# A cross-attention kernel on one core: setup and the first two batches in another order, the first keys by block products

## The chip, the core and the metric

The kernel runs on one core of one Trainium2 chip. A core has a matrix engine (TensorE, called PE in the profile; PEld is its loading of weights), VectorE (DVE), ScalarE (ACT), GpSimd (POOL), and SyncE (SP), which here only issues DMAs. [...] The metric is device microseconds of one execution, as the median of several runs.

## The reference, cut to what matters

Sixteen batches; x has 100 rows of 640, ctx_768 has 722 rows of 384, the last four of them "ca" tokens. All data is float32.

```python
query = hidden_states @ Wq                     # 100 x 640
keyt = enc @ Wk                                # 718 x 640
valt = enc @ Wv
hs = _mha(query, keyt, valt)                   # 8 heads of 80
ca_q1 = jnp.einsum('btc,th->bch', ca, Wq_ca)
ca_q1 = ca_q1[:, indices, :]                   # 100 rows picked
ca_hs1 = _mha(ca_q1, residual, residual)
ca_q2 = ca_hs1 @ Wq
ca_k2 = ca @ Wk_ca
ca_v2 = ca @ Wv_ca
ca_hs2 = _mha(ca_q2, ca_k2, ca_v2)
out = hs + ca_hs2
out = out @ Wout + b_out
out = out + residual
```

So there is a main attention over 718 rows, and a second one that goes through two small attentions.

## The kernel before, in words

**Block products.** The context's 718 rows are three thirds of 240 columns (u), each with three chunks of 128 features (c); a weight has three chunks and two halves (g). Keys (all but the last 128 columns, which go the plain way) and values of a batch are 3 x 3 x 2 blocks, made not by 18 products but by 15: each product f takes one sum of input blocks ("form" f, a_form) and one sum of weight blocks (W_AT), adds into a PSUM bank A to E, and what the bank then holds is copied (ACT) or added (DVE, L390) to one output block (`Blocks.go`, L381). V_PLAN and K_PLAN are the orders. `enc_sums` (L466) makes the input sums, thirteen operations on POOL for each batch. `weight_sums` (L487) makes the weight sums once, twelve operations; the five "late" ones overwrite raw weight blocks, or build on those. `Keys` and `Values` are the two uses.

**Batch 0 is special.** Its keys are made plainly, by `first_keys` (L561: four chunks of nine products, and the last chunk by `last_keys`, L568), and its values too, by `first_values` (L353), for the six blocks (i) of 120 rows. Values 1, 4, 2, 5 are made in the setup, values 3 and 0 within batch 0.

**Setup (L243 to L1080).** SP loads the context of batch 0 (`load_first`), the tokens (cat, wkca), the transposed query weight wqt, xT, the key weight wkt (five DMAs), the query weight wq (five) and wvca. PE makes first values, k2_ps (tokens' keys), m_ps (five), y_ps of batch 0, the transposes of wkt into w_ps, which DVE and ACT copy in turn to wk_sb, the keys of batch 0, va_ps (tokens' values, sent to DRAM as va_d), and the queries of batches 0 and 1 (`queries`, L515, five chunks). The second attention of a batch is the class `Second` (L703): `products` (y_ps and g), `scores1` (four products and three sums of 100x800 on POOL, into e1), `softmax1` (DVE), `exponentials1` (ACT), `softmax2` (z_ps on PE), `scores2`, `softmax3` (DVE), `load` (values vb, by POOL's DMA queue), `values2` (four products and three sums on POOL, into hs2).

**A batch (L1089 on).** `scores` in three groups of two blocks, copied by ACT into st (the first and third group sit in PSUM pairs of tag ps2, the second in psk and ps1); `most`, the largest, on DVE; `Maximum` (its steps are called by `top.go`); the values of this batch and the keys of the next, block by block, with `subtract` (DVE, 120x1600) and `exponential` (ACT) among them; `last_keys` of the next batch (L568); `a_ps`, probabilities by values, on PE; then normalisation on DVE. `Last` projects finished rows of 128 with wout: most batches end with one projection (o_ps, L923), and batches 0, 1, 5, 10 and 14 have none in that place. Odd batches also make the queries of the next two.

**What sets the order.** From L1088 on a manual schedule holds: each of the five engines gets its instructions in the order in which they are written. Ahead of it the framework's scheduler orders instructions by its own model of when their inputs are ready, within the limits given by `in_order` and `issue_after`. Tiles of one tag share buffers, and a new one waits until the last reader of the old is done.

Of the kernel before, what the change touches and what calls it, by code (L numbers as in the profile page):

```python
# [8 lines left out]
F32 = mybir.dt.float32  # L9
AF = mybir.ActivationFunctionType  # L10
ALU = mybir.AluOpType
# [113 lines left out]
def kernel(  # L125
# [84 lines left out]
    def rest_tile(name):  # L210
        return main.tile([P, len(A_REST), KT], F32, tag="rest", name=name)
# [11 lines left out]
    def load_rest(b, enc):  # L223
        rest = rest_tile(f"rest_{b}")
        for (u, c), i in A_REST.items():
            nc.sync.dma_start(
                out=rest[:, i], in_=enct[b][:, c, u * (KT - 1) : u * (KT - 1) + KT]
            )
        return enc[0], rest
# [44 lines left out]
    load_first(0, CC, 1, slice(KN, KT))  # L274
    for u in (2, 0):
        load_first(0, CC, u, slice(0, KT))
    tokens = vb_tile("tokens")
    cat_sb = tokens[:, CC, : CC * B * T].rearrange("p (c n) -> p c n", c=CC)
    wkca_sb = tokens[:, :CC, :]
    in_order(nc.sync.dma_start(out=cat_sb, in_=cat.rearrange("p c b t -> p c (b t)")))  # L280
    in_order(nc.sync.dma_start(out=wkca_sb, in_=wkca.rearrange("(c p) n -> p c n", p=P)))
    wqt_sb = wout_sb
    wkt_sb = kT.rearrange("p c u k -> p c (u k)")
    in_order(nc.sync.dma_start(out=wqt_sb, in_=wqt.rearrange("(c p) r -> p c r", p=P)))
    xT = inp.tile([P, 2, HC, S], F32, tag="xT", name="xT_0")
    in_order(nc.sync.dma_start(out=xT, in_=xt[0:2].rearrange("b p c s -> p b c s")))
    for c in range(HC):
        in_order(nc.sync.dma_start(out=wkt_sb[:, c, :CAD], in_=packed(wkt, c)))  # L288
# [197 lines left out]

    def weight_sums(engine, w, late):  # L487

        at = lambda f: w[:, W_AT[f]]
        raw = lambda c, g: w[:, 2 * (c - 1) + g - 1]  # L490
        for out, left, right in (
            (at(5), raw(2, 2), raw(1, 2)),
            (at(14), raw(2, 1), raw(2, 2)),
            (at(7), raw(3, 2), at(5)),
            (at(3), raw(1, 1), at(7)),
            (at(13), raw(3, 1), at(7)),
        ) if late else (
            (at(0), raw(1, 2), raw(1, 1)),
            (at(1), raw(2, 1), raw(3, 1)),
            (at(2), raw(1, 1), raw(2, 2)),  # L500
            (at(6), raw(2, 1), raw(1, 1)),
            (at(10), raw(3, 1), raw(2, 2)),
            (at(11), raw(2, 2), raw(3, 2)),
            (at(12), raw(3, 2), raw(3, 1)),
        ):
            engine.tensor_tensor(out, left, right, ALU.subtract)  # L506

# [6 lines left out]

    def queries(p, xT, tiles, n):  # L515
        qp, qz = tiles
        q_ps = psum(f"q_ps_{p}_{n}")
        for c in range(HC):
            nc.tensor.matmul(  # L519
                q_ps[:, : 2 * S].rearrange("p (j s) -> p j s", j=2),  # L520
                wq_sb[:, c, n * P : (n + 1) * P],
                xT[:, :, c, :],
                start=(c == 0),
                stop=(c == HC - 1),
            )
# [12 lines left out]
    def chunk_keys(n, banks, weights, enc):  # L538
# [20 lines left out]
        return copies  # L559

    def first_keys(enc):  # L561
        for n in range(HC - 1):
            banks = [psum(f"kT_ps_0_{n}_{k}") for k in range(2)]
            weights = [wk_sb[:, 2 * c + n % 2, n // 2] for c in range(CC)]
            chunk_keys(n, banks, weights, enc)
        last_keys(0, enc)

# [123 lines left out]
    def keys(m):  # L691

        for c, (_, groups) in enumerate(GROUPS):
            at = [i for i, h in enumerate(groups) if h >= 0]
            n, step = len(at), at[1] - at[0]
            nc.gpsimd.tensor_tensor(
                m2[:, c, at[0] : at[-1] + 1 : step, :],
                m(c).unsqueeze(1).to_broadcast([P, n, HT]),
                hmask[:, c, :n].unsqueeze(2).to_broadcast([P, n, HT]),
                ALU.mult,  # L700
            )

    class Second:  # L703


        def __init__(self, b, xT):
            self.b, self.xT = b, xT[:, b % 2]
            self.top = None

            self.ca = small.tile([S, T, S], F32, tag="ca", name=f"ca_{b}", bufs=2)  # L710
# [153 lines left out]
    class Last:  # L864
# [51 lines left out]
        def project(self, chunks=range(HC)):  # L916
            for r, xn in self.xn.items():
                lo, n = OC[r]
                if chunks[0] == 0:
                    self.o_ps = pair(f"o_ps_{r}")  # L920
                o_ps = self.o_ps
                for c, k in [(c, k) for k in range(2) for c in chunks]:
                    nc.tensor.matmul(  # L923
                        o_ps[:n, k, : H // 2],
                        hsTs[r][:, c, :n],
# [7 lines left out]
                if self.split:  # L933
                    for k in range(2):
                        cols = slice(k * (H // 2), (k + 1) * (H // 2))
                        nc.vector.tensor_tensor(
                            xn[:n, cols], o_ps[:n, k, : H // 2], xn[:n, cols], ALU.add
                        )
# [3 lines left out]
                nc.vector.tensor_tensor(both, o_ps[:n, :, : H // 2], both, ALU.add)  # L942
                nc.sync.dma_start(out=o_v, in_=xn[:n])
# [46 lines left out]
    for n, heads in enumerate(HEADS):  # L990
# [9 lines left out]
            ALU.mult,  # L1000
        )
    for c in range(HC):
        m_ps = psum(f"m_ps_{c}")
# [13 lines left out]
        nc.sync.dma_start(out=m_d[c], in_=m_sb[c])  # L1017
    second = Second(0, xT)
    keys(load_m(0))
    summed = second.products()  # L1020
    second.copy()
    second.scores1()
    keys(load_m(1))

    for c in range(HC):
        w_ps = psum(f"w_ps_{c}")
        for cc in range(CC):
            nc.tensor.transpose(
                w_ps[:, cc * P : (cc + 1) * P], wkt_sb[:, c, cc * P : (cc + 1) * P], ident
            )  # L1030
        (dve if c % 2 else act)(
            wk_sb[:, c % 2 : 6 : 2, c // 2] if c < HC - 1 else wk4,
            w_ps[:, : CC * P].rearrange("p (a n) -> p a n", a=CC),
        )

    with tc.issue_after(summed.ins):
        for c in range(HC):
# [11 lines left out]
            )  # L1049
    first_keys(enc)  # L1050

    va = wide("va")[:, : H // 2]
    va_ps = psum("va_ps")
    for c in range(CC):
# [10 lines left out]
    for n in range(2):  # L1065
# [3 lines left out]
        )  # L1069
    with tc.issue_after(copied.ins):  # L1070
        nc.vector.tensor_reduce(
            qmask, ident.rearrange("p (r u k) -> p u r k", r=RG, u=2), AX.XY, ALU.add
        )
    tiles = queries_tiles(0)
# [6 lines left out]
    engines = {  # L1081
        mybir.EngineType.Pool,
        mybir.EngineType.PE,
        mybir.EngineType.DVE,
        mybir.EngineType.Activation,
        mybir.EngineType.SP,
    }
    ctx.enter_context(tc.manual_schedule(engines=engines))  # L1088
    for b in range(B):  # L1089
# [63 lines left out]

        if b == 0:
            now.scores2()
            now.softmax3()
            second.scores1()
            top.go(3)
            kk.go(3)
            top.go(1)  # L1160
# [16 lines left out]
            subtract(2)  # L1177
            exponential(2)
            now.values2()
            second.load()  # L1180
            second.softmax1(4)
        elif b + 1 < B:
# [6 lines left out]

            second.scores1(seen)  # L1190
            last.load()
            top.go(3)
# [31 lines left out]
        else:  # L1224
# [23 lines left out]
            last.project()  # L1248
        if b + 2 < B:
            if b == 0:  # L1250
                enc_next = load_rest(b + 2, enc_next)
            keys(m_next)
            enc_sums(enc_next)
# [97 lines left out]
```

## Time and profile before

| what | value |
| --- | --- |
| median of 3 runs | 962.16 us (961.81 to 964.65) |
| the profiled execution: time, span | 964.32 us, 962.6 us |
| granted TensorE clock, mean | 0.995 |
| start of scores, batches 0, 1, 2 | 67.6, 111.2, 172.5 us |
| start of scores, batches 5, 6 | 342.4, 399.3 us |
| last matmul, end of span | 958.7, 962.6 us |
| DMA in the first 40 us | 0.73 to 0.97 of the engines' time |

The time from one start of scores to the next is the length of a batch, and PE is busy in nearly all of it from batch 2 on. The profile gives for each group of instructions the idle time of the engine ahead of it, and what ended it; "<- ACT st L1119" reads: until ScalarE's instruction of line 1119, which wrote st, was done.

### The profile page before, as it was taken

The page shows a single profiled execution, that of the slowest core. Times are in us where ns is not written, and L with a number is a line of the kernel's source. Part 1 is how long each engine was busy: PE and PEld are TensorE (multiplying, and loading weights), DVE is VectorE, ACT ScalarE, POOL GpSimd, SP SyncE. Part 2 cuts the span into 40 slices and gives each one's busy share as a digit, 9 for nine tenths or more (in the row PEclk, how much of TensorE's full clock was granted, in tenths as well). Part 3 has the DMA queues.
Part 4 walks back from the last instruction along what each step waited for, and adds up shares of the span by engine and source line. Part 5 has one row for each costly group of instructions (what it writes and reads, how often), then busy time and mean ns, then how long its engine had stood idle before and what let it go on. Part 6 is the DMA issues. An engine that isn't in the chain of part 4 may idle for free.

```text
span 962.6 us, 25608 instructions
## 1 busy us (share of the span) xinstructions
PE 941.2 (98%) x11215; PEld 799.9 (83%) x11215; DVE 673.1 (70%) x1083; ACT 359.1 (37%) x596; POOL 632.9 (66%) x572
## 2 busy tenths in 40 slices
PE   8898989999999999999999999999999999999998
PEld 6797869888798798978889787897879878898866
DVE  1357796696947869496874959569694786928883
ACT  1124433433424443342434334243432444325351
POOL 4269999485955768487673958738695576836613
PEclk9899999999999999999999999999999999999999
DMA  7930304022040301304050040401204031120100
GB/s 247 280 120 4 99 1 134 3 56 75 1 148 2 92 24 49 89 1 128 1 142 9 1 129 1 134 3 46 70 3 147 2 95 35 49 80 1 59 8 29
DMA packets 45256, 62.48 MB, mean 65 GB/s; under 512 B 13337, under 2 KB 37209, under 8 KB 43545
## 3 DMA queue, kind: packets, MB, share of 16 engines
q1 hardware_dynamic: 41608, 42.97, 15.1%
q0 software_dynamic: 2512, 16.72, 6.1%
q8 instruction: 88, 1.44, 0.6%
q10 hardware_dynamic: 1024, 1.15, 0.3%
q14 instruction: 24, 0.19, 0.1%
HBM read 55.26 MB, written 5.57 MB: 63 GB/s over the span
## 4 chain that ended last, share of the span: by engine, by line
PE 93%; DVE 2%; SPq 2%; DMA 2%; ACT 1%; issue 1%; ACTq 0%; DVEq 0%
PE s_ps L598 12%; PE a_ps L1272 11%; PE v_psA L419 10%; PE v_psB L419 8%; PE kT_ps L543 8%; PE k_psA L450 7%; PE q_ps L519 7%; PE o_ps L923 7%; PE k_psB L450 6%; PE v_psC L419 3%; PE k_psC L450 3%; PE v_psD L419 2%; PE v_psE L419 2%; PE y_ps L721 2%; PE k_psE L450 1%; SPq L288 1%
## 5 line engine op out<-in xcount | busy, mean ns | idle before, releaser
L756 POOL TENSOR_TENSOR e<-ca,g 100x800 f32<-100x800 f32 x64 | 99.3, 1562 | 155.4 <-DVE most L1123 118.7
L845 POOL TENSOR_TENSOR hs<-vb,p 100x640 f32<-100x640 f32 x64 | 105.6, 1660 | 42.5 <-DVE p L831 40.0
L1272 PEld LDWEIGHTS a_ps<-vs,st 120*64 120x64 f32 (+3 forms) x3072 | 109.1, 125 | 10.9 <-ACT st L1119 5.4
L852 POOL TENSOR_TENSOR hs<-hs,hs 100x640 f32<-100x640 f32 x48 | 115.3, 2402 | 3.8
L1272 PE MATMUL a_ps<-vs,st 120*64 120x81 f32 (+3 forms) x3072 | 112.5, 234 | 4.9 <-ACT st L1119 4.9
L419 PE MATMUL v_psA<-wv_sb,enc 128*120 128x320 f32 x360 | 113.2, 437 | 2.6 <-DVE wv_sb L506 2.6
L485 POOL TENSOR_TENSOR enc<-enc 128x240 f32<-128x240 f32 x135 | 103.9, 784 | 7.1
L1111 DVE TENSOR_TENSOR st<-st,over 120x1600 f32<-120x1600 f32 x48 | 108.0, 2253 | 0.0
L598 PE MATMUL s_ps<-qp,kT 32*120 32x100 f32 x3072 | 98.8, 263 | 0.7 <-issue 0.7
L598 PEld LDWEIGHTS s_ps<-qp,kT 32*120 32x120 f32 x3072 | 95.8, 179 | 2.5 <-issue 1.1
L763 POOL TENSOR_TENSOR e<-e,e 100x800 f32<-100x800 f32 x48 | 95.2, 1983 | 3.8
L615 ACT COPY st<-s_ps 120x800 f32<-120x800 f32 x64 | 49.7, 829 | 128.0 <-PE s_ps L598 128.0
L419 PE MATMUL v_psB<-wv_sb,enc 128*120 128x320 f32 x300 | 93.5, 434 | 0.0
L450 PE MATMUL k_psA<-enc,wk_sb 128*128 128x240 f32 x360 | 87.9, 367 | 2.5 <-DVE kT L390 1.4
L1283 DVE RECIPROCAL rs<-a_ps 100x4 f32<-100x4 f32 x32 | 5.8, 181 | 117.3 <-PE a_ps L1272 117.1
L419 PEld LDWEIGHTS v_psA<-wv_sb,enc 128*120 128x120 f32 x360 | 65.0, 184 | 26.0 <-issue 3.7
L450 PEld LDWEIGHTS k_psA<-enc,wk_sb 128*128 128x128 f32 x360 | 68.2, 190 | 19.9 <-DVE kT L390 1.9
L1123 DVE TENSOR_TENSOR most<-most,st 120x800 f32<-120x800 f32 x64 | 65.6, 1025 | 22.3 <-ACT st L609 21.2
L1119 ACT ACTIVATE st<-st 120x1600 f32<-120x1600 f32 x48 | 74.0, 1543 | 11.4 <-DVE st L1111 11.4
L419 PEld LDWEIGHTS v_psB<-wv_sb,enc 128*120 128x120 f32 x300 | 55.2, 184 | 22.5 <-issue 0.7
L450 PE MATMUL k_psB<-enc,wk_sb 128*128 128x240 f32 x300 | 73.0, 366 | 0.0
L485 POOL TENSOR_TENSOR enc<-enc,rest 128x240 f32<-128x240 f32 x45 | 34.7, 772 | 57.9 <-DMA rest<-in_enct 22.7
(138 smaller groups left out, 1762.5 us busy)
## 6 DMA issues: line engine op xcount, KB each, us to landing
vb<-va_d POOLq DMA_DIRECT2D x16, 1000.0 KB, 7.6
enc<-in_enct SPq DMA_DIRECT2D x30, 240.0 KB, 3.7
enc<-in_enct SPq DMA_DIRECT2D x15, 360.0 KB, 3.5
xT<-in_xt SPq DMA_DIRECT2D x8, 500.0 KB, 4.6
rest<-in_enct SPq DMA_DIRECT2D x31, 120.0 KB, 6.5
xn<-in_x SPq DMA_DIRECT2D x11, 320.0 KB, 9.2
out<-xn SPq DMA_DIRECT2D x11, 320.0 KB, 2.4
ca<-in_cas SPq DMA_DIRECT2D x16, 156.2 KB
```

Source lines behind the costliest of these rows:

```text
L419: nc.tensor.matmul(at[0][j][:KN, : H // 2], a_form(self.enc, f)[:, j * KN : (j + 1) * KN], wv_sb[:, W_AT[f]], start=first, stop=last, skip ...
L450: nc.tensor.matmul(at[:, i * KT : (i + 1) * KT], wk_sb[:, W_AT[f], i], a_form(self.enc, f), start=(first and i == 0), stop=last, skip_grou ...
L485: nc.gpsimd.tensor_tensor(out, left, right, op)
L543: nc.tensor.matmul(bank[:, i * KT : (i + 1) * KT], weights[c], a_raw(enc, u, c), start=(i == 0 and c == 0), stop=(c == CC - 1), skip_group ...
L598: nc.tensor.matmul(s_ps[r][:n, 256 * a + lo : 256 * a + hi], kT[rows, c, u, j * KN : (j + 1) * KN], rhs, start=(a == 0 and c == 0), stop=( ...
L756: first = nc.gpsimd.tensor_tensor(to, self.ca[:, t, :].unsqueeze(1).to_broadcast([S, NH, S]), g[:, :, t].unsqueeze(2).to_broadcast([S, NH, ...
L763: nc.gpsimd.tensor_tensor(e, e, to, ALU.add)
L845: first = nc.gpsimd.tensor_tensor(to, vb[:S, t, :].rearrange("p (h d) -> p h d", h=NH), p2[:, :, t].unsqueeze(2).to_broadcast([S, NH, D]), ...
L852: nc.gpsimd.tensor_tensor(sums, sums, to, ALU.add)
L1111: return nc.vector.tensor_tensor(st[i], st[i], top.over[:KN].unsqueeze(1).to_broadcast([KN, 2, ROWS]), ALU.subtract,)
L1119: nc.scalar.activation(st[i], st[i], AF.Exp, scale=SCALE)
L1272: nc.tensor.matmul(a_v[lo:hi, h % 4], st[i // 2][: KEYS[i], i % 2, h * S + lo : h * S + hi], block(i, h // 4)[: KEYS[i], h % 4], start=(i ...
```

## The change

- **Keys of batch 0** are made by `Keys(0, enc)`, the 15 block products, instead of `first_keys`: three, then va_ps, then four, then two behind each of the first four chunks of the queries; `last_keys(0)` comes ahead of the fifth chunk. The manual schedule begins ahead of them. Queries of batch 0 and va_ps use PSUM pairs.
- For this the encoder sums of batch 0 come in the setup on POOL, ahead of `scores1(0)`, and all twelve sums of key weights come on DVE ahead of the copies of the query weight, in a new order. The copies of w_ps are all ACT's. ca_0 is loaded ahead of wkt.
- **First values 0** move from batch 0 to the setup, ahead of m_ps; their context third is loaded behind cat and wkca.
- **Value weight sums**: the seven early ones go from POOL to DVE, ahead of batch 0's softmax1; the five late ones from DVE in batch 1 to POOL in batch 0.
- **Batch 0's order**: scores1 of batch 1 earlier, scores2 and softmax3 later, the mask products (`keys`) and the late sums ahead of values2, which now waits for the third subtract. The load of vb for batch 1 moves into batch 1. The rest blocks of batch 1's context get a buffer of their own kind (hsT).
- **Every batch to 14**: the third exponential is issued ahead of the last keys' copies.
- **The last output** (`split`) uses two PSUM tiles, one for each half.

```diff
     def load_rest(b, enc):
-        rest = rest_tile(f"rest_{b}")
+        if b == 1:
+            room = hsT_tile("rest_1").rearrange("p c s -> p (c s)")
+            rest = room[:, : len(A_REST) * KT].rearrange("p (i k) -> p i k", k=KT)
+        else:
+            rest = rest_tile(f"rest_{b}")
...
-    for u in (2, 0):
-        load_first(0, CC, u, slice(0, KT))
+    load_first(0, CC, 2, slice(0, KT))
...
     in_order(nc.sync.dma_start(out=wkca_sb, in_=wkca.rearrange("(c p) n -> p c n", p=P)))
+    load_first(0, CC, 0, slice(0, KT))
...
     in_order(nc.sync.dma_start(out=xT, in_=xt[0:2].rearrange("b p c s -> p b c s")))
+    ca_0 = small.tile([S, T, S], F32, tag="ca", name="ca_0", bufs=2)
+    in_order(nc.sync.dma_start(out=ca_0, in_=cas[0].unsqueeze(0).to_broadcast([S, T, S])))
...
-    def weight_sums(engine, w, late):
+    def weight_sums(engine, w, late=None):
...
+        for f, left, right in (
+            (0, raw(1, 2), raw(1, 1)),
+            (11, raw(2, 2), raw(3, 2)),
+            (12, raw(3, 2), raw(3, 1)),
+            (5, raw(2, 2), raw(1, 2)),
+            (7, raw(3, 2), at(5)),
+            (13, raw(3, 1), at(7)),
+            (1, raw(2, 1), raw(3, 1)),
+            (3, raw(1, 1), at(7)),
+            (6, raw(2, 1), raw(1, 1)),
+            (10, raw(3, 1), raw(2, 2)),
+            (2, raw(1, 1), raw(2, 2)),
+            (14, raw(2, 1), raw(2, 2)),
         ):
-            engine.tensor_tensor(out, left, right, ALU.subtract)
+            if late is None or late == (f in (5, 7, 13, 3, 14)):
+                made = engine.tensor_tensor(at(f), left, right, ALU.subtract)
+        return made
...
                 if chunks[0] == 0:
-                    self.o_ps = pair(f"o_ps_{r}")
+                    if self.split:
+                        self.o_ps = [bank(f"o_ps_{r}_{k}") for k in range(2)]
+                    else:
+                        self.o_both = pair(f"o_ps_{r}")
+                        self.o_ps = [self.o_both[:, k] for k in range(2)]
...
+    first_values(0, enc, (act, act))
     for c in range(HC):
         m_ps = psum(f"m_ps_{c}")
...
-    second = Second(0, xT)
-    keys(load_m(0))
+    second = Second(0, xT, ca_0)
+    made_keys = keys(load_m(0))
     summed = second.products()
     second.copy()
-    second.scores1()
+    with tc.issue_after(made_keys.ins):
+        enc_sums(enc)
+        second.scores1()
     keys(load_m(1))
...
-        (dve if c % 2 else act)(
+        act(
...
     with tc.issue_after(summed.ins):
+        made = weight_sums(nc.vector, wk_sb)
+
+    with tc.issue_after(made.ins):
         for c in range(HC):
...
-    first_keys(enc)
+    tiles = queries_tiles(0)
+    ctx.enter_context(tc.manual_schedule(engines=engines))
+    k0 = Keys(0, enc)
+    k0.go(3)
     va = wide("va")[:, : H // 2]
...
+    k0.go(4)
     for n in range(HC):
-        queries(0, xT, tiles, n)
+        queries(0, xT, tiles, n, bank)
+        k0.go(2)
+        if n == HC - 2:
+            last_keys(0, enc)
+    weight_sums(nc.vector, wv_sb, False)
...
         if b == 0:
+            enc_sums(enc)
             now.load()
             now.softmax1()
-            for late in (False, True):
-                weight_sums(nc.vector, wk_sb, late)
-            enc_sums(enc)
-            weight_sums(nc.gpsimd, wv_sb, False)
...
-        if b == 1:
-            weight_sums(nc.vector, wv_sb, True)
...
         if b == 0:
+            second.scores1()
+            kk.go(3)
+            top.go(3)
             now.scores2()
-            now.softmax3()
-            second.scores1()
-            top.go(3)
-            kk.go(3)
             top.go(1)
             first_values(3, e_in, (act, act), (0,), bank)
             kk.go(2)
             top.go()
             first_values(3, e_in, (act, act), (1,), bank)
             kk.go(3)
-            first_values(0, e_in, (act, act), (0,), bank)
+            now.softmax3()
             kk.go(2)
             subtract(0)
             exponential(0)
-            first_values(0, e_in, (act, act), (1,), bank)
             kk.go(2)
             subtract(1)
             kk.go(3)
             exponential(1)
             second_next, enc_next, m_next = loads()
+            less = subtract(2)
+            exponential(2)
             last_keys(b + 1, enc)
-            subtract(2)
-            exponential(2)
-            now.values2()
-            second.load()
+            enc_next = load_rest(b + 2, enc_next)
+            keys(m_next)
+            weight_sums(nc.gpsimd, wv_sb, True)
+            now.values2(less)
+            enc_sums(enc_next)
             second.softmax1(4)
...
             second.scores1(seen)
+            if b == 1:
+                now.load()
             last.load()
...
             subtract(2)
+            exponential(2)
             last_keys(b + 1, enc)
-            exponential(2)
```

More of the change, by code (lines that the diff above doesn't have):

```diff
@@ L485, in enc_sums @@
             nc.gpsimd.tensor_tensor(out, left, right, op)
-    def weight_sums(engine, w, late):
+    def weight_sums(engine, w, late=None):
         at = lambda f: w[:, W_AT[f]]
         raw = lambda c, g: w[:, 2 * (c - 1) + g - 1]
[L491 to L504, printed above, removed]
-        ):
-            engine.tensor_tensor(out, left, right, ALU.subtract)
+        for f, left, right in (
[11 more added lines that the diff above has]
+            (14, raw(2, 1), raw(2, 2)),
+        ):
+            if late is None or late == (f in (5, 7, 13, 3, 14)):
+                made = engine.tensor_tensor(at(f), left, right, ALU.subtract)
+        return made
     def queries_tiles(p):
@@ L513, in queries_tiles, with queries @@
         ]
-    def queries(p, xT, tiles, n):
+    def queries(p, xT, tiles, n, get=psum):
         qp, qz = tiles
-        q_ps = psum(f"q_ps_{p}_{n}")
+        q_ps = get(f"q_ps_{p}_{n}")
         for c in range(HC):
@@ L559, in chunk_keys @@
         return copies
[L561 to L566, printed above, removed]
     def last_keys(b, enc):
@@ L695, in keys @@
             n, step = len(at), at[1] - at[0]
-            nc.gpsimd.tensor_tensor(
+            made = nc.gpsimd.tensor_tensor(
                 m2[:, c, at[0] : at[-1] + 1 : step, :],
@@ L701, in keys, with __init__ @@
             )
+        return made
     class Second:
-        def __init__(self, b, xT):
+        def __init__(self, b, xT, ca=None):
             self.b, self.xT = b, xT[:, b % 2]
             self.top = None
+            self.ca = ca
+            if ca is not None:
+                return
             self.ca = small.tile([S, T, S], F32, tag="ca", name=f"ca_{b}", bufs=2)
@@ L923, in project @@
                     nc.tensor.matmul(
-                        o_ps[:n, k, : H // 2],
+                        o_ps[k][:n, : H // 2],
                         hsTs[r][:, c, :n],
@@ L936, in project @@
                         nc.vector.tensor_tensor(
-                            xn[:n, cols], o_ps[:n, k, : H // 2], xn[:n, cols], ALU.add
+                            xn[:n, cols], o_ps[k][:n, : H // 2], xn[:n, cols], ALU.add
                         )
@@ L941, in project @@
                 both = xn[:n].rearrange("p (k d) -> p k d", k=2)
-                nc.vector.tensor_tensor(both, o_ps[:n, :, : H // 2], both, ALU.add)
+                nc.vector.tensor_tensor(
+                    both, self.o_both[:n, :, : H // 2], both, ALU.add
+                )
                 nc.sync.dma_start(out=o_v, in_=xn[:n])
@@ L1049 @@
             )
-    first_keys(enc)
+    with tc.issue_after(copied.ins):
+        nc.vector.tensor_reduce(
+            qmask, ident.rearrange("p (r u k) -> p u r k", r=RG, u=2), AX.XY, ALU.add
+        )
+    engines = {
+        mybir.EngineType.Pool,
+        mybir.EngineType.PE,
+        mybir.EngineType.DVE,
+        mybir.EngineType.Activation,
+        mybir.EngineType.SP,
+    }
+    tiles = queries_tiles(0)
+    ctx.enter_context(tc.manual_schedule(engines=engines))
+    k0 = Keys(0, enc)
+    k0.go(3)
     va = wide("va")[:, : H // 2]
-    va_ps = psum("va_ps")
+    va_ps = bank("va_ps")
     for c in range(CC):
@@ L1069 @@
         )
[L1070 to L1074, printed above, removed]
-    for n in range(HC):
-        queries(0, xT, tiles, n)
+    k0.go(4)
+    for n in range(HC):
+        queries(0, xT, tiles, n, bank)
[3 more added lines that the diff above has]
+    weight_sums(nc.vector, wv_sb, False)
     nc.gpsimd.dma_start(out=bias, in_=bout[0].partition_broadcast(P))
@@ L1080 @@
     last, enc_next, second_next = None, load_rest(1, load_enc(1)), Second(1, xT)
[L1081 to L1088, printed above, removed]
     for b in range(B):
@@ L1248 @@
             last.project()
-        if b + 2 < B:
-            if b == 0:
-                enc_next = load_rest(b + 2, enc_next)
+        if 0 < b < B - 2:
             keys(m_next)
```

## The prediction, made before the changed kernel was run

> **What bounds the kernel now.** I read the engines' busy time first, then the list of waits of TensorE (PE), then the chain of waits around batches 0 and 1, then time windows there. The page's first part:
>
> ```profile
> PE 941.2 (98%) x11215; PEld 799.9 (83%) x11215; DVE 673.1 (70%) x1083; ACT 359.1 (37%) x596; POOL 632.9 (66%) x572
> ```
>
> PE is idle for only 962.6 - 941.2 = 21.4 us. A change that leaves the batches' matmuls alone can win only those holes, what PE does needlessly, and time at a low clock. The list of waits (total us, times, longest) says where the holes are:
>
> ```profile
> PE a_ps L1272 <- ACT st L1119: 4.9, 3, 1.6
> PE v_psA L419 <- DVE wv_sb L506: 2.6, 1, 2.6
> PE w_ps L1028 <- DMA kT<-in_wkt: 2.4, 1, 2.4
> PE m_ps L1005 <- DMA wout_sb<-in_wqt: 1.8, 1, 1.8
> PE k_psA L450 <- DVE kT L390: 1.4, 1, 1.4
> ...
> PE k_psA L450 <- ACT kT L392: 1.1, 1, 1.1
> ```
>
> All are in the setup and batches 0 and 1, but for two of the three a_ps waits: in the timeline these stand before 675.24 and 905.26, in two even batches that have neither queries nor an output projection between the last keys and the probabilities' product. The rest is the start and the end. The chain (start, us, step) around the two holes that matter most:
>
> ```profile
> 36.56 20.71 PE kT_ps L543 x90
> 57.27 1.77 PE va_ps L1056 x12
> 59.04 8.65 PE q_ps L519 x50
> ...
> 102.48 0.25 ACT kT L554
> ...
> 103.30 1.45 ACT st L1119
> ...
> 104.79 6.41 PE a_ps L1272 x175
> ...
> 120.46 2.79 DVE wv_sb L506 x3
> ...
> 123.38 1.92 PE v_psA L419 x3
> ```
>
> The setup ends in 31 us of unbroken PE work. Then the last exponential of batch 0 starts only when ACT has copied the last keys (102.48 to 103.30). In batch 1 PE waits for three sums of value weights on DVE. What that wait costs beyond itself is in the windows (PE busy, PEld, DVE, ACT, POOL, then the granted clock):
>
> ```profile
> 122.00:124.00 2.00, 0.62 (x1) 0.47 (x2) 1.97 (x3) 0.00 (x0) 1.84 (x3) 0.75 0.00 0
> 124.00:126.00 2.00, 2.00 (x5) 1.25 (x4) 1.97 (x6) 0.20 (x1) 2.00 (x3) 0.50 0.00 0
> ```
>
> After 2.63 us of idleness PE runs at half clock: v_psA takes 2.46 us for four matmuls and v_psB 1.64, where batch 2 has 1.26 and 1.24. That is 1.6 more.
>
> **The change part by part.** I count against the profiled execution: span 962.6 us, 964.32 with what lies around it. The median of the timed runs is 962.16, so 2.16 lower; I take the change of the span off that median.
>
> *Batch 1.* The late value-weight sums (five, 0.95 us each on DVE, row L506) leave batch 1's DVE for batch 0's POOL, behind five mask products and ahead of values2. From one start of scores to the next, batch 1 takes 111.19 to 172.55 = 61.36 us; batch 5, with the same parts (queries, no projection), 342.38 to 399.25 = 56.87. The difference, 4.49, is 2.63 + 1.6 and small change. I take -4.4. Cover: on POOL the five cost about 0.85 each, done by about 102, and batch 1 needs them from 120 on. What is late next is POOL's own queue: values2 of batch 0 now waits for the third subtract. It ends some 10.7 us after that (104.38 to 115.09 in the row), then seven encoder sums take 6.6 (119.00 to 125.6): 102.9 + 17.3 = 120.2, while PE asks for that form 13 us after the scores of batch 1 begin, at about 124. It is covered by 3.7 us. The move of vb's load (7.6 us to land) behind scores1 in batch 1 makes values2 there end near 158 + 7; its sum is first needed at 170, so nothing.
>
> The clock weighs here. [...]
>
> *The exponential ahead of the last keys' copies (every batch to 14).* Third subtract of the first quiet batch: 667.98 to 670.46; ACT then idles 3.08 us for kT_ps and copies until 673.64, and the exponential ends at 675.2. Moved ahead it ends at 670.5 + 1.55 = 672.05, before a_ps starts at 672.83. The 1.64 us go, in two batches: -3.3. The copies come at most 1.5 us later and are read by scores 6.9 us on. Bound: 0 if a PSUM buffer turns out to hang on them, though no projection follows in these batches.
>
> *The end.* The last two adds wait for all of o_ps: 958.72 and 0.89 us for both. With two banks the first half is done three matmul pairs earlier and its add runs under them, so the second store leaves one add earlier: 0.44. I take -0.4 (bounds 0 and -0.9).
>
> *Setup, to the first scores.* Removed: 72 key matmuls of the first four chunks for 60 in 15 products, -12 x 0.203 = -2.43. The six matmul pairs of first_values(0) (2 x 1.61) come in ahead of m_ps, where PE waits 1.78 for wqt and later 2.44 for wkt: 3.22 into 4.22. Added ahead of the keys: ca_0's 160 KB on SP before wkt, 0.5 at some 300 GB/s; and weight sums before the first product. Transposes end at 35.9, so the last needed copy at 36.4; five sums until form 7 at 0.41 = 2.05: PE starts at 38.5, not 36.56. From there 12.15 + 1.77 + 8.65 + 3.65 = 26.2. Today's 90 key matmuls take 20.71 against 5 x 3.65 = 18.25 at full clock, so a cold start costs 2.4; I keep it (bounds 0 and 2.4: the gap is now 2.1 us; 1.78 kept the clock, 2.44 lost it). One bank is reused after a single product: 0.3. Scores start at 67.4, where they start at 67.62.
>
> Whether form 7 is there rests on POOL: masks end at about 31.6, seven sums of 0.7 end at 36.9 if DVE leaves it alone. Two POOL sums under today's DVE weight sums took 5.20 together, one 4.36 alone. So the start can slip by up to 2.2. [...]
>
> *Batch 0.* It loses first_values(0) (3.2 on PE) and twelve sums on DVE, but DVE sets it. In the new order DVE has, after the last add of batch 0's keys (38.5 + 22.7 + 0.8 = 62.0), seven value-weight sums. They cost 0.42 (0.34 by size) to 0.95 (row); near the middle, 4.6 in all: 66.6. Then softmax1: 57.60 to 66.52 in the row less 1.16 of waiting for va_d, now earlier, = 7.8: 74.4 (today 66.5). Behind it on ACT stand the exponential (1.0) and the four copies of the second scores (1.68): 77.1. PE waits some 2 to 3 us for their banks before z_ps. DVE goes on with larger (2.5), z (0.75), larger (2.4): 82.7, today 79.98. From there to the third subtract's end today 22.7; new: maximum 3.4, scores2 1.3, two adds 1.4, wait for spread 0.8, transpose 1.0, three adds 2.1, softmax3 0.7, subtracts 3 x 2.24, four adds 2.8 = 20.2. It ends at 102.9, the exponential at 104.5, where a_ps now gets it at 104.74. So setup and batch 0 together: -0.2, bounds +6 (start 2.2, sums 2.1, subtracts at the row's worst 2.87 1.9) and -5 (clock 2.4, sums 1.6, subtracts 1.3). The bias load moved to POOL's queue (0.57 on POOL) and rest_1 in hsT's room (waits for the second mask products, near 58) lie before encoder sums which are needed at 80. On SP wout, xT and ca go behind rest_1; none is needed before 80.
>
> Sum: -4.4 - 3.3 - 0.4 - 0.2 = -8.3; span 954.3, median 953.9.
>
> **Rivals.** *The vector queue slips* (18%): sums and subtracts on DVE at their contended prices, a late form 7, so batch 0 ends 4.5 later: 958.4. For it: POOL is now full where DVE runs its sums. Against: the five sums and wkt's twelve are out of batch 0's way.
>
> *A hole moves* (12%): the copies behind the exponential hold a bank, or form 7 of batch 2 comes late in batch 1 by some 3 us: 957. Against it the 3.7 us of cover; for it that values2 now waits for the subtract.
>
> *POOL starves, slower than before* (7%): thirteen encoder sums must be done before the fifteen products are. They end at about 42 by the row; the tenth product, which wants the last of them, comes near 53.5. To lose the 8.1 us of the other parts it must come after 61.6, that is six sums at 4.1 us each from 37 on. One did take 4.36. If all six do and scores1 follows late, batch 0 slides by 11: 965. Below 4 us each it costs less than the rest wins.
>
> **How the numbers follow.** The forecast, 953.9, has 63%, with 951 to 957 as its own range. To hold 8 in 10 I go from 950.5 (the clock kept, cheap sums) to 959 (vector queue). Under 0.3%, 2.9 us here, is what a measurement can't tell from none: 959.3 to 965.0. That takes the first rival's upper end and part of the last: same 0.08, slower 0.07, faster 0.85.
>
> **What would show it.** Right: no wait of v_psA for wv_sb, clock 1.00 at the start of batch 1, batch 1 near 57 us; no a_ps wait near 665 and 895; first products near 38.5; a wait of z_ps in batch 0; a_ps of batch 0 near 104.5. Wrong: a_ps of batch 0 later than 109, or PE waiting for enc on POOL.

## The result, and the profile after

The changed kernel is slower: 968.43 us median (967.56 to 968.94) against 962.93 (961.81 to 964.65) for the kernel before on the same chip. The ratio on record is 1.0047, with a 95% interval of 1.003 to 1.0063; it is not the quotient of the two medians, which is 1.0057. The profiled execution took 967.56, its span is 965.6 and its mean granted clock 0.989, where the kernel before had 964.32, 962.6 and 0.995.

From one start of scores to the next (PE's first s_ps of each batch in the two timelines), in us:

| stage | before | after | difference |
|---|---|---|---|
| start to the scores of batch 0 | 67.62 | 80.48 | +12.86 |
| batch 0 | 43.50 | 40.95 | -2.55 |
| batch 1 | 61.36 | 58.52 | -2.84 |
| the two quiet batches | 50.32, 50.25 | 48.41, 48.40 | -3.76 |
| other batches 2 to 14 | | | -0.14 |
| last batch and end | 51.01 | 50.45 | -0.56 |

The sum is +3.0, as the spans have it. (The medians differ by 5.5: the profiled execution of the kernel before lies above its median, that of the changed kernel below.) What was meant to be won after the first scores was won in sum, 9.9 us, though batch 1 fell short of its part; the setup lost more. Engine by engine (busy us, share, count):

```profile
PE 940.3 (97%) x11203; PEld 798.0 (83%) x11203; DVE 690.3 (71%) x1092; ACT 361.7 (37%) x596; POOL 635.2 (66%) x583
```

PE is idle for 965.6 - 940.3 = 25.3 us where it was 21.4. DVE is busier by 17.2 us with nine more instructions. Some 12.9 of it, counted instruction by instruction, is work that has only become longer: the twelve sums of key weights (6.1 to 13.0) and the fifteen copies of wq (4.0 to 9.9). PE's waits (total, times, longest):

```profile
PE k_psA L456 <- DVE wk_sb L512: 6.9, 1, 6.9
PE k_psA L456 <- DVE kT L396: 6.7, 3, 4.7
PE w_ps L1041 <- DMA kT<-in_wkt: 2.1, 2, 1.8
PE a_ps L1291 <- ACT st L1142: 1.1, 1, 1.1
...
PE k_psA L456 <- POOL enc L491: 0.7, 1, 0.7
```

The old holes are closed: v_psA waits for no wv_sb, and of the three a_ps waits the one of batch 0 is left. Two new ones stand above them, both of the first key product's bank and both behind DVE. The chain of waits there (start, us, step) is DVE alone:

```profile
35.99 12.16 DVE wk_sb L512 x12
48.15 1.75 DVE wq_sb L1054 x2
49.90 1.82 DVE wq_sb L1061
...
53.61 2.07 DVE wq_sb L1054 x2
...
56.89 0.58 DVE kT L396
57.47 0.14 issue
57.61 1.94 PE k_psA L456 x4
```

Twelve weight sums, fifteen copies of wq and then the add for which PE waits: one queue. POOL's timeline at the same time (start, us, operation, count):

```profile
33.29 3.29 POOL L491 TENSOR_TENSOR enc<-enc 128x240 f32<-128x240 f32 x5
36.54 1.71 POOL L491 TENSOR_TENSOR enc<-enc,rest 128x240 f32<-128x240 f32 x2
...
45.82 2.05 POOL L767 TENSOR_TENSOR e<-e,e 100x800 f32<-100x800 f32 x1
47.95 1.60 POOL L760 TENSOR_TENSOR e<-ca,g 100x800 f32<-100x800 f32 x1
```

POOL is never idle there. Windows show the price on PE (PE, PEld, DVE, ACT, POOL busy, clock, DMA share, GB/s), and that the value products of batch 1, from 130.9 on, now run at full clock:

```profile
40.00:42.00 2.00, 0.00 (x0) 0.00 (x0) 2.00 (x3) 0.00 (x0) 2.00 (x2) 0.50 0.37 141
44.00:46.00 2.00, 1.77 (x5) 1.01 (x5) 2.00 (x3) 0.34 (x1) 2.00 (x4) 0.50 0.02 9
54.00:56.00 2.00, 0.00 (x0) 0.00 (x0) 2.00 (x5) 0.00 (x0) 1.33 (x1) 0.97 1.09 378
60.00:62.00 2.00, 2.00 (x7) 1.81 (x7) 0.90 (x2) 0.00 (x0) 1.84 (x4) 0.50 1.03 399
132.00:134.00 2.00, 2.00 (x9) 1.28 (x7) 1.93 (x3) 1.62 (x4) 1.92 (x2) 1.00 0.00 0
```

In the kernel before POOL stood still in just this stretch, for a load:

```profile
45.43 3.04 POOL L756 TENSOR_TENSOR e<-ca,g 100x800 f32<-100x800 f32 x2 [14.13 <-DMA ca<-in_cas]
```

That wait of 14.13 us cost nothing, and it kept POOL away from DVE. Loading ca_0 early and putting the encoder sums there fills it.

### The profile page after: what moved, and what is told of

Its sections match the earlier page's. It is cut to its first block, busy times and chain, and to the rows that moved or that the text cites. A ratio compares the mean times of both kernels' runs of the same rounds, so it can differ in the third digit from the quotient of the medians.

```text
span 965.6 us, 25616 instructions
## 1 busy us (share of the span) xinstructions
PE 940.3 (97%) x11203; PEld 798.0 (83%) x11203; DVE 690.3 (71%) x1092; ACT 361.7 (37%) x596; POOL 635.2 (66%) x583
## 4 chain that ended last, share of the span: by engine, by line
PE 88%; POOL 4%; DVE 3%; DMA 3%; issue 1%; SPq 1%; ACT 0%; ACTq 0%; POOLq 0%
PE s_ps L598 11%; PE a_ps L1291 11%; PE v_psA L425 10%; PE v_psB L425 8%; PE k_psA L456 7%; PE q_ps L526 7%; PE o_ps L931 7%; PE k_psB L456 6%; PE kT_ps L550 6%; PE v_psC L425 3%; PE k_psC L456 2%; PE v_psE L425 2%; PE v_psD L425 2%; PE y_ps L725 2%; DMA kT<-in_wkt 1%; PE k_psE L456 1%
## 5 line engine op out<-in xcount | busy, mean ns | idle before, releaser
L856 POOL TENSOR_TENSOR hs<-hs,hs 100x640 f32<-100x640 f32 x48 | 115.1, 2398 | 3.8
L491 POOL TENSOR_TENSOR enc<-enc 128x240 f32<-128x240 f32 x144 | 106.4, 754 | 7.1
L456 PE MATMUL k_psA<-enc,wk_sb 128*128 128x240 f32 x384 | 95.8, 373 | 14.3 <-DVE wk_sb L512 6.9
L456 PEld LDWEIGHTS k_psA<-enc,wk_sb 128*128 128x128 f32 x384 | 73.4, 193 | 33.5 <-POOL enc L491 8.5
L767 POOL TENSOR_TENSOR e<-e,e 100x800 f32<-100x800 f32 x48 | 92.2, 1922 | 3.7
L456 PE MATMUL k_psB<-enc,wk_sb 128*128 128x240 f32 x320 | 78.9, 370 | 0.6 <-DVE sm L832 0.3
```

The lines of the kernel that those rows point to most:

```text
L456: nc.tensor.matmul(at[:, i * KT : (i + 1) * KT], wk_sb[:, W_AT[f], i], a_form(self.enc, f), start=(first and i == 0), stop=last, skip_grou ...
L491: nc.gpsimd.tensor_tensor(out, left, right, op)
L767: nc.gpsimd.tensor_tensor(e, e, to, ALU.add)
L856: nc.gpsimd.tensor_tensor(sums, sums, to, ALU.add)
```

## The experiments

The theory to test: the setup is lost because POOL's two-input operations hold DVE's sums and copies up. Its rivals are that the block products themselves cost too much, that only one kind of POOL's work matters, or that the loss lies in the order of DVE's queue alone. The ratio is always to the kernel before on the same chip, as recorded.

### e1: batch 0's keys plain again

The rest of the changed kernel stays; the key-weight sums run behind the first softmax.

```diff
-        enc_sums(enc)
...
-        made = weight_sums(nc.vector, wk_sb)
...
-    k0 = Keys(0, enc)
-    k0.go(3)
+    for n in range(HC - 1):
...
+        chunk_keys(n, banks, weights, enc)
+    last_keys(0, enc)
...
             now.softmax1()
+            weight_sums(nc.vector, wk_sb)
```

> The changed kernel with one part undone: batch 0's keys are made plainly again (four chunks of nine products, then the last chunk) and no encoder sums are made for batch 0; the twelve key-weight sums stand behind batch 0's softmax1. All else is as changed. Theory A (the sums of keys and encoder blocks collide on DVE and POOL in the setup, and that is the whole loss): scores of batch 0 start near 67, not 80.5, and the span falls by at least 10, to 954 to 956. Theory B (the loss comes from the other setup edits: loads in another order, ca_0 ahead of the key weight, first values ahead of m_ps): scores still start near 78 and the span stays above 963. Theory C (batch 0's new order is at fault): the start is near 67, but batch 0 takes over 45 us.

Measured: 954.21 us, ratio 0.9905 (0.9888 to 0.9922), scores start at 63.23. So all that the setup lost comes with the block products and the sums that they need there, and the rest of the change is worth some 9 us. Not all was right: the scores start 4 us earlier than expected, and batch 1 took 63.29. POOL had waited 16.6 us for rest_1, loaded on SP's queue behind va, which the plain keys pushed to 52.8; it then ran late and PE waited 2.3 us for the encoder sums of batch 2.

### e2 to e5: POOL's two pieces of work taken away one by one

e2 puts scores1(0), all but its first product, behind the last copy of wq; e3 does so too, and runs the encoder sums of batch 0 as soon as its ctx is loaded; e5 moves only the encoder sums. With the changed kernel these are the four corners.

```diff
     first_values(0, enc, (act, act))
+    enc_sums(enc)                       # e3, e5
...
     with tc.issue_after(made_keys.ins):
-        enc_sums(enc)                   # e3, e5
-        second.scores1()                # e2, e3
...
-            nc.vector.tensor_copy(
+            parted = nc.vector.tensor_copy(      # e2, e3: the last wq copy
...
+    second.scores1(parted)              # e2, e3: behind it
```

> The changed kernel; the second attention's score products of batch 0 on POOL (all but one of them) wait for the last copy of the query weight on DVE. Theory A: the encoder sums still meet the first weight sums, so the twelve take about 8 us and not 12.2; the fifteen copies of the query weight run alone in 3.5 us and not 8.9; the second PE wait (4.7 us for the keys' sum) goes. Scores of batch 0 start near 72 to 73, the span is 957 to 960. Theory B: DVE is slow for another reason (the weight sums depend on each other, or the copies wait for their load), so the sums still take 12 and the copies near 9, the span stays at 965.

> The changed kernel with batch 0's encoder sums on POOL ahead of the mask products (in the hole of POOL before 26 us) and the score products behind the last copy of the query weight. So DVE has its weight sums and copies to itself. Theory A: twelve sums in 4.9 us, copies in 3.5, the first block product near 38.5, scores of batch 0 near 67 to 68, as the prediction had it; span 953 to 956, faster than both kernels. If the block products among the queries are themselves dear (bank reuse, low clock), scores start at 70 or later and the span is above 958.

> The fourth corner: batch 0's encoder sums early as in e3 (done by about 22), but the products of the first scores left where the changed kernel has them, so that only these run on POOL beside DVE's weight sums and copies. Theory A (any two-input operation of POOL holds DVE's two-input sums and its copies up): twelve sums take 7 to 10 us instead of 4.12, fifteen copies 7 to 12 instead of 2.8, the first key product starts at 39 to 42, the third add waits behind the copies so PE waits for kT some 3 to 6 us; scores start near 72 to 76, median 958 to 963. Rival B (only the encoder sums collide, being long and of the same kind as the weight sums): sums near 4.1, copies near 2.8, scores start near 64.7, median 953.8 as e3. If the loss of the changed kernel were a sum of two separate parts, e5 would stand above e3 by about as much as the changed kernel stands above e2: 968.4 - 959.8 = 8.6, so 962.4.

| POOL beside DVE's sums and copies | twelve sums | fifteen copies | first product | scores start | ratio (95%) |
|---|---|---|---|---|---|
| both (changed kernel) | 12.16 | 8.8 | 43.69 | 80.48 | 1.0047 (1.003 to 1.0063) |
| encoder sums (e2) | 9.03 | 4.1 | 41.24 | 70.92 | 0.9961 (0.9947 to 0.9975) |
| scores1 (e5) | 13.15 | 2.8 | 46.75 | 74.90 | 0.9996 (0.9982 to 1.001) |
| neither (e3) | 4.12 | 2.8 | 37.82 | 64.72 | 0.990 (0.9885 to 0.9915) |

The medians are 959.8 us for e2, 963.95 for e5 and, with the same instructions as the changed kernel, 953.8 for e3 (953.28 to 954.19). Theory A holds for e2 and e3, with the scores even earlier than expected. On DVE's timeline of e3 the sums and copies stand at their own price:

```profile
34.90 4.12 DVE L512 TENSOR_TENSOR wk_sb<-wk_sb 128x256 f32<-128x256 f32 x12 [1.48 <-ACT wk_sb L1042]
38.94 0.49 DVE L1052 COPY wq_sb<-wq 128x256 f32<-128x256 f32 x2
39.34 0.22 DVE L1059 COPY wq_sb<-wq 128x128 f32<-128x128 f32 x1
```

Twelve sums in 4.12 us are 0.34 each; in the changed kernel the same row is 12.16, 1.0 each, and two copies cost 1.82 instead of 0.49:

```profile
35.99 12.16 DVE L512 TENSOR_TENSOR wk_sb<-wk_sb 128x256 f32<-128x256 f32 x12 [3.18 <-ACT wk_sb L1044]
48.07 1.82 DVE L1054 COPY wq_sb<-wq 128x256 f32<-128x256 f32 x2
49.82 1.90 DVE L1061 COPY wq_sb<-wq 128x128 f32<-128x128 f32 x1
```

So the copies collide too, though they read one operand. My expectation for e5 was wrong in a useful way: I looked for sums of 7 to 10 us and slower copies, and the sums alone (13.15) lasted longer than all of scores1 that was left, so that the copies ran at their own price and the wait for them never came. Its DVE and POOL timelines show how:

```profile
35.14 3.76 DVE L512 TENSOR_TENSOR wk_sb<-wk_sb 128x256 f32<-128x256 f32 x2
36.82 3.76 DVE L512 TENSOR_TENSOR wk_sb<-wk_sb 128x256 f32<-128x256 f32 x2
```

```profile
34.89 1.72 POOL L760 TENSOR_TENSOR e<-ca,g 100x800 f32<-100x800 f32 x1
36.69 1.93 POOL L767 TENSOR_TENSOR e<-e,e 100x800 f32<-100x800 f32 x1
38.70 1.60 POOL L760 TENSOR_TENSOR e<-ca,g 100x800 f32<-100x800 f32 x1
```

(The two DVE rows overlap in one sum: the second starts at 36.82, the next at 38.83.) A sum starts a quarter of a microsecond or less after each POOL operation and ends only when the next POOL operation has begun: one sum of 0.42 us for each POOL operation of 1.6 to 1.9. POOL goes on at close to its own pace, 1.60 and 1.93 where it takes 1.54 and 1.88 alone. Here DVE, the engine with the many short operations, loses. By what mechanism the two hold each other up no run shows.

It does not always go this way. In batch 0 of the kernel before, DVE's key-weight sums met POOL's encoder sums:

```profile
66.45 3.09 DVE L506 TENSOR_TENSOR wk_sb<-wk_sb 128x256 f32<-128x256 f32 x9
...
65.74 4.36 POOL L485 TENSOR_TENSOR enc<-enc 128x240 f32<-128x240 f32 x1
```

There nine sums of DVE ran at their own price, 0.34 each, and one POOL sum, 0.69 alone, took 4.36. What decides which engine loses is not shown.

The effects nearly add up: scores1 costs 1.0047 - 0.9961 = 0.0086 beside the encoder sums and 0.9996 - 0.990 = 0.0096 without them.

### e4, e8 and e9: the other parts one at a time

e4 is the kernel before with the last exponential ahead of last_keys; e8 is the kernel before with the two separate banks at the end; e9 is e3 with the five late value-weight sums back on DVE in batch 1.

```diff
+            exponential(2)              # e4, on the kernel before
             last_keys(b + 1, enc)
-            exponential(2)
...
-            weight_sums(nc.gpsimd, wv_sb, True)      # e9, on e3
...
+        if b == 1:
+            weight_sums(nc.vector, wv_sb, True)
```

> The kernel before with one edit alone: the third exponential ahead of the last keys' copies, in batches 1 to 14. The two a_ps waits of 1.64 us in the quiet batches go, with what follows them: -3.3 to -3.9 us of span (958.7 to 959.3), as between the two profiles (50.3 to 48.4 us for each of these batches). A rival: the gain in the changed kernel came from other things, then there is no difference here.

e4: 960.11 us, ratio 0.9962 (0.9948 to 0.9977), so -3.7; the quiet batches took 48.42 and 48.41.

> The kernel before with nothing but the last output's two separate banks. From the last batch's first scores to the end of the span the kernel before takes 51.01 us, the changed kernel 50.45. Theory A (the split alone makes the end's gain): 50.4 to 50.6, every other stage as before within 0.1. Rival B (the exponential ahead of the copies, or the order of the last batch, has a share): 50.7 to 51.0.

e8, by its profile alone: last batch and end 50.49, so -0.52; the other stages are as before but for the start (68.45), batch 0 (43.87) and batch 11, which differs from run to run (62.92 here, up to 64.72 in e9). The last adds on DVE's timeline stand apart, the first under the matmuls of the second bank:

```profile
957.54 0.49 DVE L940 TENSOR_TENSOR spare<-o_ps,spare 128x320 f32<-128x320 f32 x1 [3.29 <-PE o_ps L927]
959.15 0.49 DVE L940 TENSOR_TENSOR spare<-o_ps,spare 128x320 f32<-128x320 f32 x1 [1.12 <-PE o_ps L927]
```

> e3 with one part of the change undone: the five late sums of value weights go back from POOL in batch 0 to DVE in batch 1. Theory A (the prediction's first step: these sums cost batch 1 the wait of v_psA for wv_sb and the half clock behind it, 4.4): v_psA waits 2 to 3.2 us, the clock drops to 0.50 behind it, batch 1 takes 61 to 62 us where e3 has 57.38, ratio to before 0.9935 to 0.995 where e3 has 0.990. Rival B (POOL, rid of 7 us in batch 0, starts its encoder sums earlier and DVE's sums run beside them no slower than alone, so the value weights are ready in time): batch 1 57 to 58.5, ratio 0.990.

e9: 957.01 us, ratio 0.9919 (0.990 to 0.9938). Batch 1 took 61.70, 4.32 more than in e3, as expected, but not by the steps I had named, and the ratio rose less than either step would have it (0.9935 was Theory A's least). Its waits in batch 1:

```profile
PE v_psA L425 <- DVE wv_sb L512: 1.4, 1, 1.4
PE k_psE L456 <- DVE vs L396: 1.0, 1, 1.0
PE v_psD L425 <- DVE z L798: 0.9, 1, 0.9
```

The clock stayed at 1.00 and the wait for the sums was shorter; the 4.58 us of sums on DVE push its whole queue, and PE waits in three places instead. Batch 0 became 3.68 shorter in return (39.98 against 43.66). Of that, 0.65 is the subtracts: 1.81, 2.11 and 2.18 in e3, beside POOL's value-weight sums, and 1.81, 1.82 and 1.82 in e9. The rest is about what e3 loses at half clock behind a wait of 2.64 us for kT (four products 6.39 us instead of 4 x 0.81, so 3.15), where e9 waited 2.01 and kept the clock. The changed kernel, with POOL's sums there and no half clock, took 40.95, so the move itself is worth about 1 us of batch 0 and the rest is the clock of one execution. By the ratios the move is worth 0.9919 - 0.990, some 1.8 us, and the intervals overlap.

### e6, e7, e10, e11: can it be better?

e6 is e1 with the va_ps matmuls behind the second chunk of keys; e7 is e3 with batch 0's last plain chunk ahead of the first products; e10 and e11 are e3 and e6 with scores2 behind two of batch 1's key adds.

```diff
+        chunk_keys(n, banks, weights, enc)
+        if n == 1:                      # e6
+            va = wide("va")[:, : H // 2]
...
+    last_keys(0, enc)                   # e7
     k0.go(3)
...
         k0.go(2)
-        if n == HC - 2:
-            last_keys(0, enc)
...
-            now.scores2()               # e10, e11
             top.go(1)
             first_values(3, e_in, (act, act), (0,), bank)
             kk.go(2)
+            now.scores2()
             top.go()
```

> e1 (batch 0's keys plain, key-weight sums behind the first softmax) with the twelve va_ps matmuls behind the second chunk of keys instead of behind the last. In e1 batch 1 took 63.29 us because POOL stood idle for 16.6 us for rest_1, whose load stands behind va on SP's queue, and then ran late through the whole of batch 0 (values2 to 110.3, encoder sums to 123.8 where PE asked for form 7 at 117.4). Theory A (POOL's lateness comes from there): enc_1 loads some 10 us earlier, POOL's encoder sums end near 60 and no later than 65, k_psA's wait of 2.3 for enc and the half clock behind it go, batch 1 takes 57 to 60, median 948 to 951.5. Rival B (POOL's queue in batch 0 is bound by the products that come only after the scores, near 74.9, which e1 started at 76.67): POOL gains 1.7 at most, batch 1 takes 61 to 62, median 952 to 953.

e6: 952.25 us, ratio 0.9865 (0.9837 to 0.9893), the lowest of all; its interval overlaps those of e1 and e3. POOL's encoder sums of batch 1 ended at 63 and batch 1 took 59.01, so Theory A's mechanism, though the median lies where Rival B had it: 0.7 of the 2.3 us of waiting stays. Set beside e3, e1 and e6 say one thing more. With the collision away the block products start the scores at 64.72, plain keys at 63.23 and 63.80: what the fewer matmuls save (2.43 by the forecast) goes into PE's wait of 2.76 us for the weight sums. No run's time shows a gain from the block products in this place.

> e3 with the twenty plain matmuls of batch 0's last key chunk ahead of the first products, where PE waits 2.8 us for seven weight sums. Theory A (the wait is for the sums alone, and the plain chunk needs only the transposes' last copy, near 36.4): PE waits 1.2 to 1.6 there, and the chunk's 4.06 us cover the rest; scores start 1 to 1.6 earlier than in e3 at the same landing of wkt; median 952.2 to 952.8. Rival B (the copies of the plain chunk on ACT or its two banks hold up the products behind it): no gain, 953.5 to 955.

e7: 955.36 us, ratio 0.990 (0.9872 to 0.9927). The wait for weight sums is gone, scores start at 62.75 (the chunk is 18 matmuls and 3.75 us, not twenty and 4.06), and nothing is won, for neither theory's reason: DVE's softmax1 begins no earlier (64.25, in e3 63.63), so PE meets a new wait in batch 0, which takes 45.06:

```profile
PE z_ps L787 <- ACT st L609: 2.7, 1, 2.7
```

> e3 with the second softmax's score step of batch 0 (three small operations on DVE, 1.45 us, and its exponential on ACT) behind the maximum's spread and two of batch 1's key adds instead of ahead of them. In e3 PE waited 2.64 us for the add of k_psA and ran at half clock behind it, 84.94 to 91.5: 7.18 us for four products that take 4 x 0.81 at full clock... 3.7 more; batch 0 took 43.66 where the changed kernel, with no such loss, took 40.95. Theory A (it is the length of this wait that costs the clock; e9 kept it after 2.01 there): the wait falls to 1.0 to 1.4, the clock stays at 1.00, batch 0 takes 39.5 to 41.5, ratio to before 0.986 to 0.988. Rival B (the clock falls there for another reason, as the dense work ahead of it): wait shorter by 1.4, clock still 0.50, batch 0 42 to 42.5, ratio 0.9885 to 0.989.

> The same edit on e6, which waited 1.77 us there and kept its clock. Theory A: only the wait itself can go, batch 0 39.5 to 40.0 where e6 has 40.94, ratio to before 0.985 to 0.986. Rival B (DVE's chain from the maximum to the third subtract sets batch 0, and the edit only changes its order): 40.9 again, ratio 0.9865.

e10: 955.09 us, ratio 0.9895 (0.9874 to 0.9916); batch 0 took 41.98 with the clock at 1.00. The wait of 2.64 became 1.23, but a later product then waited 1.56, so Theory A is right about the clock and not about the gain. (The four slow products of e3 took 6.39 us, not the 7.18 of the expectation.) e11: 954.63 us, ratio 0.9897 (0.9876 to 0.9917); batch 0 took 40.93, as e6, and the third subtract ended 32.91 us after the scores began in both. So Rival B of e11 is right about batch 0: behind the scores, DVE's chain to the third subtract sets batch 0, and its order alone moves the wait. Neither is told apart from e3 or e6 by its time.

## Why the prediction was wrong, point by point

**The step that failed** is the setup's weight sums: "five sums until form 7 at 0.41 = 2.05: PE starts at 38.5". The sums began at 35.99, even before the 36.4 of the forecast, and PE started at 43.69. Two things were wrong in it. The smaller one, 0.9 us: in e3, with POOL quiet, PE starts 2.92 us after the first sum, when eight are done (7 x 0.34 + 0.42 = 2.8), not five. In the changed kernel and in e2 too it starts 0.15 us after the eighth has ended. The next product needs form 13, the sixth in the text, and in the changed kernel it waited until 0.15 us after the tenth:

```profile
45.85 1.94 PE L456 MATMUL k_psB<-enc,wk_sb 128*128 128x240 f32 x4 [0.23 <-DVE wk_sb L512]
```

That fits another order of the sums on DVE than the text's, since they stand ahead of the manual schedule; the trace does not name the forms, so it is not shown. The larger one, 4.8 us, is the price: the first eight sums took 7.55 us and all twelve 12.16, instead of 2.77 and 4.12 beside an idle POOL (e3). And the fifteen copies behind them had no term at all: 8.8 us instead of 2.8, with the first add of batch 0's keys behind them. From the first product to the scores I had 28.9 us, the changed kernel 36.79; the 7.9 are about the second wait of 4.74, the half clock behind it (5.89 us for two key products and ten query matmuls that need 3.31, so 2.58) and a first stretch at half clock (0.50 in both) that cost 3.1 instead of 2.4.

Over the whole kernel the span was to change by -8.3 and changed by +3.0. Of the 11.3 between them the setup brought 13.1; batch 0 gave 2.6 back, batch 1 cost another 1.6, and the rest gave back 0.8.

I had seen the collision, and in the setup priced it for the other engine. "Whether form 7 is there rests on POOL", and the rival "POOL starves" had encoder sums at 4 us. (The forecast's seven encoder sums of 0.7 from 31.6 end at 36.5, not 36.9; nothing rests on that.) The rival "the vector queue slips" did name DVE's contended prices and a late form 7, but gave them 4.5 us and took the twelve key sums for a relief of batch 0. In the runs POOL's encoder sums of that stretch ended at 43.3, near the forecast's 42, and DVE starved. The row I used for it (two POOL sums in 5.20 under DVE's weight sums) shows that either engine can lose, but as a row in which POOL lost it was no price for DVE's loss. I let the collision slow POOL's encoder sums alone, a slip of up to 2.2 us by the row of 4.36; for DVE's sums beside scores1 the forecast of the setup had no term.

**Batch 0** was forecast at about its old length and took 40.95, 2.55 less: the seven value-weight sums cost 2.89, not 4.6, since POOL was quiet at 75, and the third subtract ended 32.9 us after the scores began, not 35.5.

**Batch 1**: -4.4 was forecast, -2.84 came, and -3.98 in e3 (57.38). In the changed kernel 0.65 of the 1.14 between the two is a wait for form 7 of batch 2, the second rival in small: the cover of 3.7 us on POOL was used up, since the five sums there took 7.47 us and not 4.3. The other 0.5 is open. e9 shows that the gain in batch 1 is real and that part of it is paid in batch 0.

**The exponential** was right in its mechanism and its bound: -3.3 forecast, -3.76 measured, -3.7 alone in e4; no bank hung on the late copies. **The end**: -0.4 forecast, -0.56 measured, -0.52 alone in e8.

Of the signs named in advance, three came: no wait of v_psA, batch 1 at full clock, no a_ps wait in the quiet batches. Two did not, the first product near 38.5 and a z_ps wait in batch 0, and the sign of being wrong did: a_ps of batch 0 went on at 115.1, by the late start alone.

The forecast's time, 953.9, is what e3 takes, with a ratio of 0.990 where the forecast's is 953.9 / 962.16 = 0.9914. That makes it no better a forecast: it is the time of another order, in which POOL's work is out of DVE's way.

## What to carry to other kernels

When work is moved onto DVE or POOL, look at what the other one runs in that same stretch and price both sides of the collision, since either can lose: in e5 a DVE sum of 0.34 cost a whole POOL operation, 1.6 to 1.9, and in the kernel before a POOL sum of 0.69 took 4.36. An idle stretch of one of the two can be what keeps the other fast, as POOL's wait of 14.13 us did here; filling it is not free: the copies of wq went from 4.0 us to 9.9. And a start that is won is worth nothing where a later chain of another engine sets the stage's end (e7: scores 1.97 us earlier than in e3, ratio 0.990 in both).

## What the runs showed of the hardware that was not expected

How long PE idles does not alone decide whether the clock falls. Before the first product e3 idled 2.76 us and e9 2.41; the windows of e3 (as above, clock third from the right) and then those of e9:

```profile
36.00:38.00 2.00, 0.18 (x1) 0.21 (x2) 2.00 (x7) 0.00 (x0) 0.00 (x0) 1.00 0.96 368
38.00:40.00 2.00, 2.00 (x11) 1.88 (x11) 2.00 (x10) 0.84 (x2) 0.00 (x0) 1.00 0.38 139
```

```profile
36.00:38.00 2.00, 0.35 (x1) 0.38 (x2) 2.00 (x7) 0.00 (x0) 0.00 (x0) 0.83 1.03 398
38.00:40.00 2.00, 2.00 (x6) 1.67 (x6) 2.00 (x10) 0.37 (x1) 0.00 (x0) 0.50 0.47 181
```

The longer gap kept the clock and the shorter one lost it, in the same place of nearly the same program. The prediction had put a threshold between 1.78 (kept) and 2.44 (lost). What else differs is how busy PE was just before: 0.98 us of the two from 34 to 36 in e3, 0.81 in e9. What decided here no run shows; the length of the gap alone does not fit these rows. One kernel's executions differ in the clock too: e11's four took 950.71 us at a mean clock of 0.999, 953.61 at 0.998, and 955.65 and 955.94 at 0.996.
